# Issuing the row renewals of a tiled map iteration from GpSimd instead of from SyncE

## The chip, the cores and the metric

The kernel runs on one core of a Trainium2 chip. The time is device microseconds of one execution, and the runs of the kernel before have a median of 9524.16 us (three runs, 9523.93 to 9524.88 us). One more execution was taken under the hardware profiler; its page and trace are what is read below.

A core has a matrix engine (TensorE, PE in the profile; its weight loads are PEld), a vector engine (DVE), a scalar engine (ACT), GpSimd (POOL) and SyncE (SP). [...] SP computes nothing here: it issues transfers.

## What is computed

The input is `x`, 8 images of 8 channels of 512 x 512 floats. There are two layers, each with a residual. Layer 0 is a small spectral convolution of the group-normalised image, layer 1 is this:

```
drive = grid = normalised x
for _ in range(15):
    mapped = 3.9 * grid * (1 - grid)
    local  = conv3x3(mapped, one 3x3 kernel per channel)
    grid   = 0.85 * (0.7 * mapped + 0.3 * local) + 0.15 * drive
cml = clip(grid)
nca = sigmoid(conv1x1(relu(conv3x3(x, 8 -> 128)), 128 -> 8))
g   = sigmoid(conv1x1(relu(conv3x3([x, cml, nca], 24 -> 8))))
out = x + g * cml + (1 - g) * nca
```

The 15 steps of the map are the part that matters here. Each step needs, for each row, the rows above and below it.

## The kernel before, in words

**The map.** An image is cut by rows into slabs of 32 rows that lie 30 rows apart (`SLAB`, `PITCH`), so neighbouring slabs share two rows. A set (class `Slabs`) holds four slabs of four channels in one tile `m` of 128 partitions: four blocks of 32 partitions by four blocks of 514 floats. One of the two block indices is the slab and the other the channel, and they change places at each step, because the convolution of a step (line 524, 48 matmuls of 32 x 32 weights) moves a block from one index to the other. A half of an image (four channels) has four sets; the second half has a fifth, `Tail`, for the last rows. The first half of an image is one phase of 60 convolutions (4 sets by 15 steps), the second half one of 75 (5 by 15): 1080 in all. Within a phase the sets take turns, so a set is convolved at every fourth or fifth place.

After a convolution `settle` finishes the step: two DVE instructions add the drive and write `m` (line 537), two ACT instructions square it (line 543). In step 1 POOL scales the even drive (line 516, called from `drive`), in step 13 POOL adds 0.5 to the odd drive (line 547).

**The renewal.** A slab's first and last rows lack a neighbour, so after each of the first 14 steps they are wrong and are fetched from the neighbouring slab (`renew`). Lines 570 and 571 are one transfer each way: row 30 of a slab becomes row 0 of the next, row 1 of the next becomes row 31 of the slab. One such pair serves the slabs within a set; a second pair serves the border to the set above, and its line 571 writes into that set's tile. In odd steps the pair within a set copies three partitions of 2056 floats, in even steps four of 1542; the pair between sets copies one partition as 8 x 257, or four of 514. The tail set has its own `renew` (lines 637, 641, 646), which is not touched.

**A turn.** `turn` emits two convolutions with the rest of the work placed around them, 540 turns for the whole map. In `work` (line 1013) the order is: POOL scales the odd drive of sets that are due (line 516); convolution A; its two DVE instructions and the first square; `others.finish()` (line 821 on DVE and the store of line 828 on SP); convolution B; the rest of A's step, with A's renewals; B's two DVE instructions and first square; the loads of `transfers`; up to two rounds of the 128-channel convolution (line 723, read out by lines 729 and 731), in the first of which B's step ends, with B's renewals; the gate's convolution (line 793, with lines 798 on POOL and 803 on DVE); its second part (line 810, the sigmoid of line 814 on ACT, and line 816 on POOL). What line 816 makes is read by line 821 in the next turn, and line 723 of that turn follows line 821.

`keep_order` (line 102) makes each engine keep the order of the source. Every transfer of the main part is issued by SP, so its list mixes the renewals with the loads and stores; SP waits in turn for whatever the next transfer needs. Each transfer also carries one of eight completion semaphores, taken in rotation[...]. POOL's list in the map holds only lines 516, 547, 798 and 816.

Of the kernel before, what the change touches and what calls it, by code (L numbers as in the profile page):

```python
# [111 lines left out]
def view(t, offset, dims):  # L112

    return bass.AP(tensor=t.tensor, offset=t.offset + offset, ap=[list(d) for d in dims])
# [3 lines left out]
def conv_layers(ctx: ExitStack, tc: tile.TileContext, a, out):  # L118
    nc = tc.nc
# [350 lines left out]
    class Slabs:  # L470
# [84 lines left out]
        def renew(self, step):  # L555
            s, width = 4 * NP, (4 if step % 2 else 1) * NP
            m, above = self.m, self.above


            if step % 2:  # L560
                pairs = [(m, 0, m, 32 * s, [[32 * s, 3], [1, 4 * NP]])]
                if above:
                    pairs.append((above.m, 96 * s, m, 0, [[s, 1], [1, 4 * NP]]))
            else:
                pairs = [(m, 0, m, NP, [[32 * s, 4], [1, 3 * NP]])]
                if above:
                    pairs.append((above.m, 3 * NP, m, 0, [[32 * s, 4], [1, NP]]))
            for ta, oa, tb, ob, dims in pairs:
                ra, rb = oa + PITCH * s, ob
                nc.sync.dma_start(out=view(tb, rb, dims), in_=view(ta, ra, dims))  # L570
                nc.sync.dma_start(out=view(ta, ra + s, dims), in_=view(tb, rb + s, dims))
            if self.k == SETS - 1:
                r, past = TAIL_AT - (4 * SETS - 1) * PITCH, self.e.past[step]
                past = past[self.c0 : self.c0 + 4]
                if step % 2:
                    past = past.rearrange("(a c) w -> a c w", a=1)
                    row = m[96 + r : 97 + r, :, 1 : N + 1]
                else:
                    row = view(m, r * s + 3 * NP + 1, [[32 * s, 4], [1, N]])
                nc.sync.dma_start(out=past, in_=row)  # L580
# [377 lines left out]
    for i in range(3):  # L958
        xn = dram.tile([NP + 1, C, N], F32, name=f"xn{i}")
        cml, nca = (dram.tile([NP, C, N], F32, name=f"{name}{i}") for name in ("cml", "nca"))  # L960
        for plane in (xn, cml, nca):
            nc.scalar.dma_start(
                out=view(plane, 0, [[(NP - 1) * C * N, 2], [N, C], [1, N]]), in_=zrow
# [185 lines left out]
```

## Time and profile before

| | |
|---|---|
| median of the runs | 9524.16 us |
| the profiled execution: its own time / its span | 9539.07 us / 9537.3 us |
| PE busy | 9076.3 us, 95% |
| DVE, ACT, POOL busy | 5572.4, 4071.8 and 1671.2 us |
| line 570, line 571 | 1568 transfers each, issued by SP, median 0.645 and 0.631 us of SP each |
| all transfers issued by SP | 7496 |
| lines 547, 798, 816 on POOL | 72, 344 and 344 instructions of 5.37, 1.28 and 1.27 us |

The span runs from the first to the last instruction of the profiled execution. Busy time of an engine does not count its waiting. [...] its busy share says how long it had something in hand, not how near it is to its peak. The time in which an engine was idle is put down to whatever released it. The transfers that SP issues show only the time that the issue held SP; the bytes move later, as packets of the queue.

### The profile page before, as it was taken

To read this page: it belongs to the slowest core of one execution; us is meant where nothing else is said; L and a number is where in the kernel's file an instruction comes from. 1 tells how busy PE (TensorE), PEld (TensorE's weight loads), DVE (VectorE), ACT (ScalarE), POOL (GpSimd) and SP (SyncE) were. 2 spreads that over 40 slices of the span, in tenths; PEclk is the share of its full clock that TensorE was granted. 3 is DMA by queue.
4 is the path that set the end of the run, shared out by engine and by line. 5 is a ranking of instruction groups with operands and counts; after the bars stand their busy time and mean duration, and the time that the engine had idled before them with its cause. 6 is when DMAs were issued, how large, how long until landed. Compare 5 with 4: busy or idle time off the path is not lost. (4 is left out here: it accounts for less than half of the span.)

```text
span 9537.3 us, 330619 instructions
## 1 busy us (share of the span) xinstructions
PE 9076.3 (95%) x148976; PEld 4075.3 (43%) x148976; DVE 5572.4 (58%) x5820; ACT 4071.8 (43%) x4285; POOL 1671.2 (18%) x1286
## 2 busy tenths in 40 slices
PE   6999999999999999999999999999999999888999
PEld 3444444444444444444444444444444444333433
DVE  5665566655665556655566555665556655454555
ACT  2444444444444444444444444444434444333432
POOL 2010111112121121211212121021211212122122
PEclk9999999999999999999999999999999999999999
DMA  4241365565555555555555546555464555565288
GB/s 146 87 127 35 90 165 137 148 142 137 157 152 142 140 130 146 160 133 136 153 135 162 146 117 172 131 158 133 120 175 131 156 142 123 138 157 139 70 203 196
DMA packets 626870, 1326.71 MB, mean 139 GB/s; under 512 B 75258, under 2 KB 80762, under 8 KB 597970
## 3 DMA queue, kind: packets, MB, share of 16 engines
q1 hardware_dynamic: 623104, 1304.42, 53.5%
q8 instruction: 1170, 19.17, 0.9%
q14 instruction: 242, 1.98, 0.1%
q10 hardware_dynamic: 2354, 1.14, 0.0%
HBM read 977.48 MB, written 270.61 MB: 131 GB/s over the span
## 5 line engine op out<-in xcount | busy, mean ns | idle before, releaser
L524 PE MATMUL pair<-m,band 32*32 32x512 f32 x103680 | 3719.4, 607 | 208.7 <-issue 124.1
L543 ACT ACTIVATE m<-m 128x1024 f32<-128x1024 f32 x2016 | 2124.5, 1055 | 2438.6 <-DVE m L537 2293.2
L723 PE MATMUL pair<-cols,w_p 32*128 32x511 f32 (+1 forms) x24576 | 2860.0, 603 | 44.8 <-ACT y L749 14.4
L524 PEld LDWEIGHTS pair<-m,band 32*32 32x32 f32 x103680 | 2005.0, 103 | 1856.4 <-issue 1052.5
L537 DVE SCALAR_TENSOR_TENSOR m<-pair,dO 128x1024 f32<-128x1024 f32 x1152 | 1356.6, 1219 | 1218.4 <-PE pair L524 973.3
L723 PEld LDWEIGHTS pair<-cols,w_p 32*128 32x128 f32 x24576 | 1310.0, 186 | 1612.4 <-issue 1158.8
L537 DVE SCALAR_TENSOR_TENSOR m<-pair,dE 128x1024 f32<-128x1024 f32 x1008 | 1187.0, 1219 | 1142.4 <-PE pair L524 902.9
L731 DVE TENSOR_SCALAR h<-pair,b_p 128x1024 f32<-128x1024 f32 x1024 | 1313.0, 1283 | 877.8 <-PE pair L723 873.4
L729 ACT ACTIVATE h<-pair,b_p 128x1024 f32<-128x1024 f32 x1024 | 1140.6, 1114 | 902.5 <-PE pair L723 902.1
L816 POOL TENSOR_TENSOR mix<-mix 96x512 f32<-96x512 f32 x344 | 438.0, 1273 | 4302.2 <-ACT mix L814 4053.3
L742 PE MATMUL pair<-h,w_u 128*32 128x512 f32 x8192 | 1059.1, 610 | 47.6 <-ACT h L729 47.5
L793 PE MATMUL pair<-gin,w_g 128*32 128x511 f32 (+1 forms) x8256 | 964.7, 600 | 4.0 <-DMA gin<-nca 2.0
L798 POOL TENSOR_TENSOR mix<-mix 96x512 f32<-96x512 f32 x344 | 442.2, 1285 | 1423.4 <-DMA mix<-nca 1134.4
L547 POOL TENSOR_SCALAR dO<-dO 128x2048 f32<-128x2048 f32 x72 | 394.5, 5491 | 1009.4 <-DVE m L537 1009.1
L742 PEld LDWEIGHTS pair<-h,w_u 128*32 128x32 f32 x8192 | 244.1, 110 | 698.1 <-issue 329.2
L755 ACT ACTIVATE y<-y,b_u 128x512 f32<-128x512 f32 x256 | 184.8, 722 | 816.9 <-DVE y L751 816.9
L793 PEld LDWEIGHTS pair<-gin,w_g 128*32 128x32 f32 x8256 | 234.5, 110 | 684.6 <-issue 463.1
L749 ACT COPY y<-pair 128x512 f32<-128x512 f32 x256 | 150.1, 586 | 634.4 <-PE pair L742 487.2
L803 DVE TENSOR_SCALAR mix<-pair,b_g 128x512 f32<-128x512 f32 x344 | 258.2, 750 | 263.0 <-PE pair L793 262.5
L810 PE MATMUL pair<-mix,w_g 128*32 128x512 f32 x2064 | 370.7, 605 | 41.9 <-DVE mix L803 38.9
L821 DVE SCALAR_TENSOR_TENSOR mix<-mix,back 96x512 f32<-96x512 f32 x344 | 313.5, 911 | 144.2 <-POOL mix L816 144.2
L516 POOL TENSOR_SCALAR dO<-dO,base 128x512 f32<-128x512 f32 x288 | 208.4, 741 | 1075.6 <-DMA dO<-xn 923.9
(87 smaller groups left out, 2632.2 us busy)
## 6 DMA issues: line engine op xcount, KB each, us to landing
gin<-xn SPq DMA_DIRECT2D x344, 384.0 KB
cols<-xn SPq DMA_DIRECT2D x256, 512.0 KB
x<-in_x SPq DMA_DIRECT2D x120, 1024.0 KB
gin<-cml SPq DMA_DIRECT2D x344, 320.0 KB
gin<-nca SPq DMA_DIRECT2D x344, 320.0 KB
dE<-xn SPq DMA_DIRECT2D x288, 256.0 KB
dO<-xn SPq DMA_DIRECT2D x288, 256.0 KB
mix<-xn SPq DMA_DIRECT2D x344, 192.0 KB
```

The source lines that it names most:

```text
L524: nc.tensor.matmul(ps[h // 2][32 * t : 32 * t + 32, h % 2], band[at, self.channel(step - 1, h, t), dx], m[at, t, dx : dx + N], start=(n == ...
L537: nc.vector.scalar_tensor_tensor(u[:, at], ps[q], FLOOR, d[:, at], ALU.max, ALU.add)
L543: nc.scalar.square(u[:, at], u[:, at])
L547: nc.gpsimd.tensor_scalar(d, d, 0.5, None, ALU.add)
L723: nc.tensor.matmul(ps[g // 2][:, g % 2, lo:hi], w_p[p, dx, i % 2], self.cols[p, i // 2, at : at + hi - lo], start=(n == 0), stop=(n == 2), ...
L729: nc.scalar.activation(h[:, :2], ps[0], AF.Relu, bias=b_p)
L731: nc.vector.tensor_scalar(h[:, 2:], ps[1], b_p, 0.0, ALU.add, ALU.max)
L742: nc.tensor.matmul(ps[32 * g : 32 * g + 32], w_u[:, r % 4], h[:, g], start=(r == self.hs[0][0]), stop=(r == self.hs[-1][0]), tile_position ...
L793: nc.tensor.matmul(ps[32 * j : 32 * j + 32, lo:hi], gband[:, dx], gin[:, j, at : at + hi - lo], start=(n == 0), stop=(n == 2), tile_positi ...
L798: nc.gpsimd.tensor_tensor(d, d, ng, ALU.subtract)
L810: nc.tensor.matmul(ps[at], gpoint[:, at], mix[:, 3], start=True, stop=True, tile_position=(0, 32 * j),)
L816: nc.gpsimd.tensor_tensor(d, d, mix[: GR * C, 2], ALU.mult)
```

## The change

Lines 570 and 571 are issued by GpSimd. What is copied, the tiles, the order in which the renewals come and all other transfers stay.

```
@@ -567,8 +567,8 @@
                     pairs.append((above.m, 3 * NP, m, 0, [[32 * s, 4], [1, NP]]))
             for ta, oa, tb, ob, dims in pairs:
                 ra, rb = oa + PITCH * s, ob
-                nc.sync.dma_start(out=view(tb, rb, dims), in_=view(ta, ra, dims))
-                nc.sync.dma_start(out=view(ta, ra + s, dims), in_=view(tb, rb + s, dims))
+                nc.gpsimd.dma_start(out=view(tb, rb, dims), in_=view(ta, ra, dims))
+                nc.gpsimd.dma_start(out=view(ta, ra + s, dims), in_=view(tb, rb + s, dims))
             if self.k == SETS - 1:
                 r, past = TAIL_AT - (4 * SETS - 1) * PITCH, self.e.past[step]
                 past = past[self.c0 : self.c0 + 4]
```

The built programs differ in two lists only: SP's loses 3136 transfers, POOL's gains them, in among lines 516, 547, 798 and 816 where the source emits them. The renewals then have eight completion semaphores of their own, and the eight of SP's transfers are left to the other 4360.

More of the change, by code (lines that the diff above doesn't have):

```diff
@@ L569, in renew @@
                 ra, rb = oa + PITCH * s, ob
-                nc.sync.dma_start(out=view(tb, rb, dims), in_=view(ta, ra, dims))
-                nc.sync.dma_start(out=view(ta, ra + s, dims), in_=view(tb, rb + s, dims))
+                nc.gpsimd.dma_start(out=view(tb, rb, dims), in_=view(ta, ra, dims))
+                nc.gpsimd.dma_start(out=view(ta, ra + s, dims), in_=view(tb, rb + s, dims))
             if self.k == SETS - 1:
```

## The prediction

> **What bounds the kernel now.** The page first: busy time of each engine, then its costliest groups.
>
> ```profile
> PE 9076.3 (95%) x148976; PEld 4075.3 (43%) x148976; DVE 5572.4 (58%) x5820; ACT 4071.8 (43%) x4285; POOL 1671.2 (18%) x1286
> ...
> L547 POOL TENSOR_SCALAR dO<-dO 128x2048 f32<-128x2048 f32 x72 | 394.5, 5491 | 1009.4 <-DVE m L537 1009.1
> ```
>
> PE has something in hand for 95% of the span. Little can be won beside it, and whatever holds PE up is lost for good. POOL is idle for 9537 - 1671 = 7866 us, but its line 547 is long: 5.5 us at a time.
>
> Next, PE's own waits.
>
> ```profile
> PE pair L524 <- issue: 124.1, 79, 4.3
> ...
> PE pair L524 <- DMA m<-m: 37.3, 9, 11.1
> ```
>
> Columns: us in total, times, longest. Renewals (`m<-m`) hold PE for 37.3 us in all: 9 waits, among them one of 2.7 to 11.1 us at the start of each of the seven later images. No other transfer holds PE in the map. That is all that faster renewals can give directly: 0.4%.
>
> One of these waits in the timeline (start, us):
>
> ```profile
> 1177.57 1.05 ACT L543 ACTIVATE m<-m 128x1024 f32<-128x1024 f32 x1
> ...
> 1178.57 0.68 SPq L570 DMA_DIRECT2D m<-m  x1
> 1179.30 1.24 SPq L571 DMA_DIRECT2D m<-m  x1
> 1180.59 0.92 SPq L570 DMA_DIRECT2D m<-m  x1
> 1181.55 1.02 SPq L571 DMA_DIRECT2D m<-m  x1
> ...
> 1187.91 3.09 PE L524 MATMUL pair<-m,band 32*32 32x512 f32 x43 [6.13 <-DMA m<-m]
> ```
>
> SP had been issuing something else until 1178.5 us (a store, line 758, that it held from 1171.0), so renewals whose data were squared at 1174.0 us left late; the last one landed 6.3 us after its issue.
>
> Elsewhere there is slack. Each renewal's packets are recognisable by size (8224, 6168, 2056 and 1028 bytes); from issue to the end of its last packet is 2.0 us at the median, 9.7 at the 99th percentile. From there to the matmul that needs it is 22 us at the median; in the phases of four sets, for the row written into the set above, 11, and under 4.3 in one case of 20.
>
> Last, the other side: what waits for POOL.
>
> ```profile
> DVE mix L821 <- POOL mix L816: 144.2, 43, 8.1
> ```
>
> And a turn of step 13, with two line 547 in a row:
>
> ```profile
> 2218.16 11.12 POOL L547 TENSOR_SCALAR dO<-dO 128x2048 f32<-128x2048 f32 x2 [3.65 <-DVE m L537]
> ...
> 2228.12 0.67 ACT L814 ACTIVATE mix<-pair,b_g 96x512 f32<-96x512 f32 x1
> ...
> 2229.25 1.27 POOL L816 TENSOR_TENSOR mix<-mix 96x512 f32<-96x512 f32 x1
> ...
> 2233.18 0.74 DVE L821 SCALAR_TENSOR_TENSOR mix<-mix,back 96x512 f32<-96x512 f32 x1
> ...
> 2234.01 2.43 PE L723 MATMUL pair<-cols,w_p 32*128 32x512 f32 x20
> ```
>
> Line 816 already starts late here (the sigmoid ended at 2228.79), and ends 2.66 us before line 821 starts. PE's line 723 comes right behind line 821, and so does convolution B's read-out on DVE: a late line 816 is a late PE.
>
> [...] this trace shows 1.1 us at least and 1.4 at the median from SP's issue to the first packet. [...] The trace has no transfer issued by POOL[...]. [...]
>
> **The change part by part.**
>
> *Taken from SP.* 3136 issues of some 0.64 us, 2.0 ms, and SP's waits for line 543 (1275.6 us at line 570). SP is on PE's path only where it is late: the 37.3 us. The loads of a turn go out about 2.6 us earlier (four issues); PE waits for none of them in the map, so nothing.
>
> *Added to POOL.* 3136 issues at c us each. The trace does not give c. From below: SP's fastest, 0.49 us[...]. [...] POOL is then busy 1671 + 3136 = 4807 us, half the span; it would be full at c = (9537 - 1671)/3136 = 2.5 us.
>
> *Line 816 behind the renewals.* Of the 540 turns, 224 have eight renewals. In a common turn they cost nothing: B's are ready near the middle of the turn (2508.7 in the turn of 2500 to 2516 us), eight at 1.0 us fit in before the sigmoid that line 816 waits for (2518.04), and line 821 leaves it another 2 us. In the quoted turn they don't fit. POOL is never idle there: 11.12 for line 547 twice, 8c, 1.27 for line 816, from 2218.16: it ends at 2230.55 + 8c, and line 821 is late by 8c - 2.63 us: 5.4 at c = 1. That goes to line 723 and PE. I laid POOL's new list, in its new order, along the trace: an instruction starts when its input is there (the end of line 543, 537 or 814, or its old start) and POOL is free, and each delay of line 821 shifts what follows. At c = 1.0, 15 of 344 executions of line 821 are late, by 47.8 us in all; over 0.5 us it is late once or twice per image, always in or behind step 13 with its line 547, by 7.4 us at most. At c = 0.5 it is 8.8 us, at 0.8, 29; at 1.2, 73; at 1.5, 151; at 2.0, 600.
>
> *Renewals behind POOL's work.* They wait for lines 516, 547, 798 and for each other: 1.35 us at the median at c = 1, 12 at the 99th percentile, inside the slack above. With 2 to 3 us from issue to landing (the old median, and 1 more), convolutions wait 7 to 10 us more, chiefly in step 14 of the last phase, where turns are short. [...] faster landing is not counted.
>
> *The waits of 37.3 us.* In the same laying-out the renewals are ready early enough to save 34 us: in the quoted case they leave POOL by 1178.2 us. Of the longest, 11.1 us, 7.8 are saved; the others go whole.
>
> *Lines 516 and 547 behind renewals.* Their outputs are needed a step or two later, one or two rounds of sets (30 us and more); lost cover would show as DVE waiting for line 516, 21.1 us now. Nothing.
>
> Sum at c = 1.0: +47.8 + 7 (to 10) - 34 = +21 to +24; some spare for what I left out, +25. On the profiled execution: 9539.07 + 25 = 9564. The runs lie 15 us below it: 9524.16 + 25 = 9549, taken as 9550.
>
> **The rivals.**
>
> *Faster: POOL's issue is as cheap as SP's.* At c = 0.5 the sum is 8.8 + 0 - 35 = -26: 9498. It decides below c = 0.7 (-10). For it: a renewal has only 3 to 8 pieces, SP needs 0.64 us. [...] At c = 0.8 the sum is 0: the change is a wash between 0.7 and 0.95.
>
> *Much slower: POOL becomes the bound.* At c = 1.5: 151 + 45 - 31 = +165, 9690; at 2.0: 599 + 135 - 23 = +711, 10235. Common turns then overflow: eight issues are 12 to 16 us of a turn of some 16. For it: nothing in the trace excludes it. [...]
>
> *No change: the renewals were hidden and stay hidden.* For it: 22 us of slack. Against: seven turns in which they were not, and line 816, which is not a renewal. The change does what it says: the built lists show it.
>
> **How the numbers follow.** A measurement of this kernel can tell about 0.2%, 19 us, from no change. Cheap issue, c under 0.7: 22%, 9490 to 9515. Wash, c of 0.7 to 0.95: 20%, 9514 to 9540. The forecast, c of 0.95 to 1.35: 43%, 9533 to 9620 (at 1.3: 90 + 23 - 33 = +80), its lowest tenth within 0.2%. Beyond 1.35: 15%. Thus faster 0.23, same 0.25, slower 0.52. The range leaves out the cheapest few per cent and those over c = 1.4 (+118 to 131): 9494 to 9645.
>
> **What would show it.** POOL busy near 4800 us, its rows for lines 570 and 571 near 1.0 us; PE's wait for `m<-m` down from 37.3 to under 12 us; DVE's wait of line 821 for line 816 up from 144 by some 50, in turns with line 547; line 828 on SP waiting as before. The forecast fails if c is not near 1.0, if landings from POOL take over 5 us[...].

## The result, and the profile after

The changed kernel takes 9490.16 us (median of 7 runs, 9478.60 to 9497.38), the kernel before beside it 9524.88 us (7 runs, 9509.79 to 9534.68). The ratio is 0.9963, 95% interval 0.9951 to 0.9974: faster by 0.37%, some 35 us. The prediction was 9550 us with a range of 9494 to 9645, so it had the sign wrong. The profiled execution took 9485.99 us, its span is 9484.2 us.

The page of the changed kernel: busy time of each engine, then groups (busy us, mean ns of one, idle before them).

```profile
PE 9052.0 (95%) x148976; PEld 4062.8 (43%) x148976; DVE 5647.2 (60%) x5820; ACT 4078.4 (43%) x4285; POOL 3362.1 (35%) x4422
...
L570 POOL DMA_DIRECT2D m<-m x1568 | 864.1, 551 | 3929.1 <-ACT m L543 3853.4
...
L571 POOL DMA_DIRECT2D m<-m x1568 | 844.9, 539 | 30.0 <-issue 25.9
...
L547 POOL TENSOR_SCALAR dO<-dO 128x2048 f32<-128x2048 f32 x72 | 391.9, 5443 | 112.4 <-DVE m L537 111.4
```

A renewal holds POOL for 0.545 us at the mean, not 1.0: POOL is busy for 1691 us more, not 3136. DVE, which the change gave nothing to do, is busy for 75 us more. Most of that is line 799, the DVE instruction that comes behind line 798 and now often runs beside it: its time over 0.73 us an instruction sums to 74.6 us in the map, 10.9 before. No wait of PE shows a loss from it, and the fastest kernel below has nearly as much of it (71.3).

The waits of the changed kernel (us in total, times, longest):

```profile
DVE mix L821 <- POOL mix L816: 152.8, 52, 9.2
...
PE pair L524 <- issue: 105.7, 72, 3.7
...
PE pair L723 <- DVE m L537: 16.4, 6, 3.3
...
PE pair L524 <- DMA m<-m: 13.5, 8, 4.0
```

PE's wait for renewals fell from 37.3 to 13.5 us. Most of line 821's wait lies after the map has ended: within the map it is 8.4 us, where no such wait is listed before. New is PE's line 723 waiting for line 537, 16.4 us (4.2 before).

The image start that the prediction showed, now from the changed kernel's timeline (start us, duration us):

```profile
1160.91 8.16 SPq L758 DMA_DIRECT2D nca<-y  x1
...
1170.00 0.54 POOL L570 DMA_DIRECT2D m<-m  x1 [0.38 <-ACT m L543]
1170.53 0.51 POOL L571 DMA_DIRECT2D m<-m  x1
...
1180.73 1.87 PE L524 MATMUL pair<-m,band 32*32 32x512 f32 x45
```

SP is held by the store of line 758 as before (8.16 us), but the renewals leave POOL 0.4 us after their square. From this convolution to the next it is 8.9 us (1171.8 to 1180.7); before it was 17.1 (1180.7 to 1197.8). Compared convolution by convolution (the start of each in one kernel against the same one in the other), the seven later image starts gain 46 us together (5.0 to 8.2 each).

The same view has what is lost, in the turn of step 13 that the prediction quoted:

```profile
2212.18 0.67 ACT L814 ACTIVATE mix<-pair,b_g 96x512 f32<-96x512 f32 x1
...
2217.56 1.28 POOL L816 TENSOR_TENSOR mix<-mix 96x512 f32<-96x512 f32 x1
...
2218.80 5.37 POOL L547 TENSOR_SCALAR dO<-dO 128x2048 f32<-128x2048 f32 x1
2218.87 4.12 DVE L821 SCALAR_TENSOR_TENSOR mix<-mix,back 96x512 f32<-96x512 f32 x1 [1.54 <-POOL mix L816]
...
2224.18 5.51 PE L723 MATMUL pair<-cols,w_p 32*128 32x512 f32 x24 [3.26 <-DVE m L537]
```

Line 816 is late behind the eight renewals, and line 821 waits 1.54 us for it: that was foreseen. Line 821 then takes 4.12 us instead of 0.74, because its late start puts it next to a line 547 on POOL: that was not. In the map this happens seven times, each time 0.07 or 0.08 us after a line 547 began. The loss is handed to PE.

Line 821 was not always short in the kernel before (durations in ns: least, median, greatest):

```profile
L821 DVE SCALAR_TENSOR_TENSOR mix<-mix,back x344: 737/739/1859, 1240.2 to 9533.1; 96x512 f32<-96x512 f32 x172
```

In 52 of the map's 301 executions it ran beside line 798, and took up to 1.86 us; in the map of the changed kernel it meets line 798 nowhere. What it takes over 0.74 us an instruction sums to 21.0 us in the map before and 25.1 after: seven long ones in place of many shorter ones.

### The profile page after: what moved, and what is told of

It reads as the page before. It is cut to its first block, busy times and chain, and to the rows that moved or that the text cites. A ratio compares the mean times of both kernels' runs of the same rounds, so it can differ in the third digit from the quotient of the medians.

```text
span 9484.2 us, 331791 instructions
## 1 busy us (share of the span) xinstructions
PE 9052.0 (95%) x148976; PEld 4062.8 (43%) x148976; DVE 5647.2 (60%) x5820; ACT 4078.4 (43%) x4285; POOL 3362.1 (35%) x4422
## 5 line engine op out<-in xcount | busy, mean ns | idle before, releaser
L723 PE MATMUL pair<-cols,w_p 32*128 32x511 f32 (+1 forms) x24576 | 2854.9, 603 | 59.8 <-DVE m L537 16.4
L570 POOL DMA_DIRECT2D m<-m x1568 | 864.1, 551 | 3929.1 <-ACT m L543 3853.4
L571 POOL DMA_DIRECT2D m<-m x1568 | 844.9, 539 | 30.0 <-issue 25.9
```

The lines of the kernel that those rows point to most:

```text
L570: nc.gpsimd.dma_start(out=view(tb, rb, dims), in_=view(ta, ra, dims))
L571: nc.gpsimd.dma_start(out=view(ta, ra + s, dims), in_=view(tb, rb + s, dims))
L723: nc.tensor.matmul(ps[g // 2][:, g % 2, lo:hi], w_p[p, dx, i % 2], self.cols[p, i // 2, at : at + hi - lo], start=(n == 0), stop=(n == 2), ...
```

## The experiments

Ratios are to the kernel before, run beside each set; its medians were 9516.89 us for the four kernels up to the longer line 547, 9526.12 for the two that follow and the two of the last pair, and 9522.94 for the two between these. The first four ran on one chip, the others on another; each kernel has 4 to 14 runs. Kernels with a new tile have their lines two further down (line 547 is 549, line 821 is 823); where the issuing engine is chosen per step, what follows it lies one further.

**Where the gain comes from: the renewals of step 1 alone, and all but those.**

```
-                nc.sync.dma_start(...)
+                q = nc.gpsimd if step == 1 else nc.sync     # first kernel
+                q = nc.sync if step == 1 else nc.gpsimd     # second kernel
+                q.dma_start(...)
```

> Only the renewals of step 1 (224 of 3136) are issued by GpSimd, the others by SP as before. Theory A, the gain is that these few leave SP's clogged queue at the start of a phase: PE's wait for m<-m falls from 37 us to under 10, and the time is 30 to 45 us under the kernel before, as good as the whole change or better, since POOL's cost in step 13 is gone. Theory B, the gain is SP's shorter list, so that loads leave earlier: 7% of the issues are moved, so 2 or 3 us.

> The reverse: step 1 stays with SP, the other 2912 renewals are issued by GpSimd. Theory A: PE's wait for m<-m stays at 30 to 40 us, POOL's cost in step 13 remains (8 us of waiting for line 816, 24 us of a longer line 821), so 0 to 25 us over the kernel before. Theory B: about 32 us under it.

Measured: step 1 alone 9486.77 us, ratio 0.9963 [0.9950, 0.9975]; the rest 9522.43 us, 1.0001 [0.9993, 1.0009]. PE's wait for renewals in the first:

```profile
PE pair L524 <- DMA m<-m: 7.9, 4, 3.7
```

and in the second:

```profile
PE pair L524 <- DMA m<-m: 51.7, 13, 10.0
```

224 of 3136 renewals, the ones at the image starts, bring as much as all of them. The reading at this point was that the other 2912 bring nothing. That was too quick, as the kernels with a short line 547 show further down: they bring two things of opposite sign.

**What POOL's time costs: twice as many issues.**

```
+                n = dims[-1][1] // 2
+                for at in (0, n):
+                    some = [*dims[:-1], [1, n]]
+                    nc.gpsimd.dma_start(out=view(tb, rb + at, some), in_=view(ta, ra + at, some))
...
```

> Each renewal is issued by GpSimd as two transfers of half the columns, so POOL pays two issues of 0.54 us, 1.09 us for what cost 0.545. This is the price that the prediction had taken. If the prediction's laying-out is right, line 821 then waits about 60 us for line 816, convolutions wait 10 to 25 us more, and the time is 35 to 60 us over the kernel before (9560 to 9585). If POOL has room for it, the time stays that of the change, 35 us under the kernel before.

Measured: 9621.09 us, 1.0105 [1.0088, 1.0123], 100 us over the kernel before and more than the laying-out gave. An issue stays at 0.55 us, POOL is busy for 5005.8 us. Waits of this kernel (line 573 and 574 issue, 821 and 826 are the former 816 and 821):

```profile
POOL m L573 <- DMA m<-m: 282.4, 194, 6.8
...
POOL m L574 <- DMA m<-m: 273.8, 234, 4.6
...
DVE mix L826 <- POOL mix L821: 267.6, 111, 8.5
...
PE pair L524 <- DMA m<-m: 59.6, 36, 5.5
```

Line 821's wait is there as the prediction describes it (124.3 us of it within the map). But POOL also waits for earlier renewals to land, 556 us in all. The trace names the semaphores: 425 of these 428 waits are for the one that the waiting issue itself carries. POOL's transfers take eight of them in turn: in the changed kernel 392 transfers carry each, and every one had landed 2.8 us or more before the next issue that carried the same. The laying-out had no such wait; so this kernel confirms the path to PE, and is no clean measure of its size.

**Line 547: longer, then shorter.** In the quoted turn POOL's renewals, line 816 and line 547 stand in one row. The first kernel was meant to shorten line 547 (theory: its one-operation form is the slow one). It takes the form for that of line 516, but subtracts where line 516 adds:

```
-                nc.gpsimd.tensor_scalar(d, d, 0.5, None, ALU.add)
+                nc.gpsimd.tensor_scalar(d, d, 1.0, mhalf, ALU.mult, ALU.subtract)
```

> The change, with line 547 written as d * 1.0 - (-0.5) with the constant in a tile, the form of line 516, which takes 2.0 us for the same 2048 floats where line 547 takes 5.4. If the form sets the duration, line 547 falls to 2.0 us, line 821 no longer waits for line 816 nor takes 4.1 us beside line 547, and the time is 10 to 25 us under the change. If the duration comes from what runs beside it, it stays at 5.4 us and the time at that of the change.

Measured: 9551.91 us, 1.0038 [1.0024, 1.0052]. This form is slower still, by the groups of that kernel:

```profile
L547 POOL TENSOR_SCALAR dO<-dO,mhalf 128x2048 f32<-128x2048 f32 x72 | 519.6, 7216 | 96.5 <-DVE m L537 94.9
```

The expectation failed, but the run tells something: 72 x 1.8 = 128 us more on an engine that is idle for two thirds of the time cost about 70 us (1.0038 - 0.9963 = 0.75%); its runs have a granted TensorE clock (as a share of full speed) of 0.980 to 0.983, against 0.984 to 0.986 with the change, which may be part of that. In the map, line 821 now takes 5.06 us ten times, each time beside a line 547. The second kernel takes exactly line 516's form:

```
+    phalf = cp.tile([P, 1], F32, name="phalf")
+    nc.vector.memset(phalf, 0.5)
...
-                nc.gpsimd.tensor_scalar(d, d, 0.5, None, ALU.add)
+                nc.gpsimd.tensor_scalar(d, d, 1.0, phalf, ALU.mult, ALU.add)
```

> The change, with line 547 written as d * 1.0 + 0.5, the 0.5 read from a 128 x 1 tile: the very form of line 516, which takes 2.0 us for 2048 floats, against 5.37 us of the form with an immediate add. Everything else as in the change. Theory C (line 547 is what the change still pays for: line 816 stands behind it and the renewals, and line 821 runs long beside it): line 547 near 2.0 us, POOL busy some 240 us less than in the change (72 x 3.4), line 821 no longer longer than 2 us anywhere, its waits for line 816 within the map near 0, and a time 15 to 40 us under the change, that is a ratio to the kernel before of 0.992 to 0.995. Rival (the change's remaining losses lie elsewhere, at the conflict of 798 with 799 or in the later landings): line 547 shorter, but the time as the change's within 10 us, ratio 0.9955 to 0.997. If line 547 does not get shorter with this form, the run says nothing on either.

Measured: **9440.05 us, ratio 0.9906 [0.9891, 0.9921]**, the fastest of all: 50 us under the change, more than expected. Line 547 in its groups:

```profile
L549 POOL TENSOR_SCALAR dO<-dO,phalf 128x2048 f32<-128x2048 f32 x72 | 150.2, 2087 | 191.8 <-DVE m L539 190.5
```

The same turn in its timeline:

```profile
2216.43 0.66 ACT L816 ACTIVATE mix<-pair,b_g 96x512 f32<-96x512 f32 x1
...
2217.18 1.27 POOL L818 TENSOR_TENSOR mix<-mix 96x512 f32<-96x512 f32 x1 [2.18 <-ACT mix L816]
...
2221.50 0.74 DVE L823 SCALAR_TENSOR_TENSOR mix<-mix,back 96x512 f32<-96x512 f32 x1
2221.69 2.39 POOL L549 TENSOR_SCALAR dO<-dO,phalf 128x2048 f32<-128x2048 f32 x1 [3.23 <-DVE m L539]
```

POOL is now idle for 2.18 us ahead of this turn's line 818 (the former 816) and ends it 3 us before it is needed; line 823 takes 0.74 us, and nowhere more than 1.74. Compared with the changed kernel convolution by convolution, the map's last one starts 39 us earlier. Seven places give 38 us of it, 3.6 to 6.9 us each: the seven turns in which the changed kernel has a line 821 of 4.12 us. The ups and downs elsewhere sum to 1 us.

**The short form without the other renewals.**

> Only the renewals of step 1 on GpSimd (224 of 3136, the rest on SP), with the same form of line 547 as in the run before. Theory C holds that line 547 costs time only where renewals stand between it and line 816; in this kernel the step-13 renewals are SP's, so 0 to 10 us under the kernel with step 1 alone: ratio to the kernel before 0.995 to 0.9965. Rival (a line 547 of 5.4 us costs by itself, through the vector engine beside it, also without renewals on POOL): over 15 us under it, ratio under 0.995.

> The kernel before, all renewals on SP, with only the form of line 547 changed (2.0 us in place of 5.37). Theory C (line 547's length costs only where renewals stand between it and line 816): 0 to 10 us under the kernel before, ratio 0.999 to 1.0005. Rival (the 50 us that this form took off the change come from line 547 itself, wherever the renewals are issued): 30 to 50 us, ratio 0.995 to 0.997.

> The other 2912 renewals (all but step 1's) on GpSimd, with the short form of line 547. With the long form these renewals gave nothing (ratio 1.0001). Theory D (they gave two things that cancelled: a gain of some 40 us over the whole map and stalls of line 821 in the turns of step 13): with the stalls gone the gain shows, ratio 0.9945 to 0.997, although PE's wait for renewals stays near 50 us because step 1 is still SP's. Rival (they give nothing by themselves, and the best version needs all renewals off SP): ratio above 0.998.

Measured: with step 1 on GpSimd 9485.22 us, 0.9944 [0.9926, 0.9961]; with all renewals on SP 9512.44 us, 0.9990 [0.9980, 0.9999]; with all but step 1 on GpSimd 9480.50 us, 0.9956 [0.9944, 0.9969]. The short form takes 10 us off the kernel before, as theory C expects where no renewals stand on POOL. What it takes off the kernel with step 1 alone is less certain: 1.5 us by the medians, 18 by the ratios. The ratio 0.9944 lies in the rival's range and its interval reaches into theory C's; two of the six runs (9449.36 and 9465.93 us) lie 17 us and more under the others. The run with all renewals on SP decides between the two. And the other renewals do bring a gain once the long line 547 is out of their way. Together with the others:

| on GpSimd | line 547 as it was (5.4 us) | short form (2.0 us) |
|---|---|---|
| none | 1 | 0.9990 |
| step 1 (224) | 0.9963 | 0.9944 |
| all but step 1 (2912) | 1.0001 | 0.9956 |
| all (3136) | 0.9963 | 0.9906 |

Read downwards, step 1 is worth 0.37 to 0.50% (35 to 48 us) in every pairing. The other 2912 are worth nothing with the long line 547, and 0.34 to 0.38% (32 to 36 us) with the short one. Read across, the short form is worth 0.10 to 0.19% where the other renewals are SP's, 0.45 to 0.57% where they are POOL's: the stalls in the step-13 turns cost the difference, some 35 us. So the change holds three terms: about -35 (image starts), about -35 (the other renewals), about +35 (step 13). Single entries are uncertain by 0.1 to 0.2%, so the terms are good to 10 to 20 us.

What the -35 of the other renewals is made of is not settled. With step 1 still on SP, PE's wait for renewals does not fall:

```profile
PE pair L526 <- DMA m<-m: 45.4, 11, 10.3
```

The gain is spread over the map. PE's idle time without a visible cause is 20 us less than with the short form alone (131.3 to 110.9 us). Its busy time is 20 us less too (9059.4 to 9039.5 us), but the granted clock was 0.986 in place of 0.983 in these two executions; if it followed the clock, the ratio of the clocks alone would give some 28 us (an estimate: 9059.4 x 0.003 / 0.986), so the busy time tells nothing. Among runs at a clock of 0.984 the gain is 25 us (median 9511.0 us of 5 runs, 9486.0 of 2).

The traces hold one candidate. With the short form alone, line 821 is lengthened beside line 798, as in the kernel before, by 20.7 us in the map; with the other renewals ahead of line 798 in POOL's list the two no longer meet, and it is 1.3 us. The 27 turns in which line 821 lost over 0.3 us gain 15 of the 38 us by which the map is shorter. As many turns picked at random gain 4 us on average and now and then 25, so this is a hint; no run separates it.

**Why step 1's renewals were late: the store, SP's list, or something shared.** Here those of step 1 go to ACT's list, which is not SP's either, and then only the store of line 758 goes to GpSimd:

```
+                q = nc.scalar if step == 1 else nc.sync     # first kernel, lines 571 and 572
...
-                    nc.sync.dma_start(                      # second kernel, line 758
+                    nc.gpsimd.dma_start(
```

> Only the renewals of step 1 are moved, and to the scalar engine's queue instead of GpSimd's: again a list that is not SP's[...]. Theory A1 (what the seven image starts gained is the place in line: the renewals no longer stand behind a store and bulk loads in SP's list): the wait of PE for renewals in the map falls to 8 to 12 us as with step 1 on GpSimd and the ratio is 0.996 to 0.998, the scalar engine losing 224 x 0.65 = 146 us of its idle time, some of it ahead of line 543's squares. Rival A2 [...]: at the image starts the scalar engine's issues take several us each, the wait of PE for renewals stays above 25 us, and the ratio is 0.999 or more.

> The kernel before, all renewals on SP, but the store of line 758 (which held SP for 6.6 to 7.5 us at four of the seven image starts) issued by GpSimd. Theory S1 (that store holds SP because of what it itself waits for or how many pieces it has; without it SP is free for the renewals): at those four starts the renewals leave at their squares' ends, the wait of PE for renewals falls from 37 to some 15 to 22 us, ratio 0.997 to 0.9985. Rival S2 (SP's list is held [...], and whatever comes next is held): the next issue after the loads takes 6 to 7 us in its place, the waits stay at 30 us or more, ratio 0.9995 to 1.001.

Measured: ACT 9626.44 us, 1.0103 [1.0088, 1.0118]; the store 9528.90 us, 1.0003 [0.9995, 1.0011]. Neither theory foresaw the first: PE's wait for renewals fell as one has it, to 5.3 us, and yet the kernel lost 100 us. PE now waits for ACT (lines 743 and 730 are the former 742 and 729; this wait was 47.5 us before):

```profile
PE pair L743 <- ACT h L730: 133.9, 117, 18.4
...
PE pair L524 <- DMA m<-m: 5.3, 2, 5.2
```

Its timeline at one image start:

```profile
2343.26 0.69 ACTq L571 DMA_DIRECT2D m<-m  x1
...
2351.91 0.68 ACTq L572 DMA_DIRECT2D m<-m  x1
...
2355.61 0.67 ACTq L571 DMA_DIRECT2D m<-m  x1
2356.32 0.64 ACTq L572 DMA_DIRECT2D m<-m  x1
2357.01 2.00 ACT L543 ACTIVATE m<-m 128x1024 f32<-128x1024 f32 x2 [15.85 <-DMA m<-m]
```

An issue takes 0.7 us, but ACT stands still for 8 us between two of one pair, and for 3 us more before the next; ACT is idle for 15.85 us ahead of the square behind them. What it waits for can be read from the trace, which names the semaphores. ACT's and SP's transfers carry the same eight, those of GpSimd eight others. In the kernel before, SP's 7496 issues take theirs in turn, 936 to 938 each, and 7319 of them stand behind a wait for the very one that they carry. The issue at 2351.91 carries the one that a store of SP's (line 601, the former 600), issued at 2333.41, had carried before it, and starts 0.02 us after the last update of that semaphore, so after the store's landing. The issue at 2355.61 starts in the same way 0.02 us after the landing of a gate load of SP's, issued at 2344.71. In all, ACT waits 25 times for the semaphore that its own issue carries, 67.4 us together; every wait of over 2.6 us is one for a transfer of SP's.

Three image starts lose 13.6 to 16.2 us at one convolution, 45 us together, and win some of it back just after. The starts of seven second phases lose 4.8 to 15.3 us, 63 together; there the waits for semaphores are 2.6 us at most, and what else ACT's issues delay is not worked out. SP's own hold does not reach ACT: while SP's store of line 759 (the former 758) was held for 8.35 us from 2334.73, ACT issued two renewals at 2336.09 and 2336.86, in 0.74 and 1.25 us.

The second, SP's timeline where before line 758 had been held for 7.83 us behind the stores of line 600 (the expectation counts four such image starts; they are six of the seven, with 6.6 to 7.8 us):

```profile
2325.17 7.88 SPq L600 DMA_DIRECT2D cml<-m  x6
2333.15 6.81 SPq L570 DMA_DIRECT2D m<-m  x1
```

With the store gone, the next in the list, now a renewal, is held for 6.81 us; at the seven image starts it is 2.9 to 7.4 us. So it is what stands ahead of it, line 600, that holds SP; the store was only next in line. How these stores hold SP is not shown. PE's wait stays:

```profile
PE pair L524 <- DMA m<-m: 35.9, 8, 11.0
```

## Why the prediction was wrong

**The step that failed** is the cost c of an issue on POOL. The forecast is worked out at c = 1.0 us. That was the author's estimate; the trace of the kernel before has no transfer issued by POOL and did not show it. How long the issue holds POOL and when the transfer's packets move are two different things. POOL was held for 0.545 us at the mean, less than SP before (0.60). The first packet of a renewal came 1.07 us after the issue at the least and 2.4 at the median, and its last packet ended 3.6 us after the issue at the median (3.0 for line 570, 4.3 for line 571), against 2.0 from SP. The rival "Faster: POOL's issue is as cheap as SP's" was the true case; its price, 9498 us, is 8 us from the median. With c = 0.545 the prediction's own figures, read between those for 0.5 and 0.8, give about 12 us of stalls and 35 saved: -23 against the measured -35 (interval -25 to -47). That this comes so near is in part luck, as what follows shows.

**It does not follow that the rest of the working was right.** Two terms were missing, and they cancel.

- *"PE waits for none of them in the map, so nothing"* (SP relieved of 2912 renewals): with the short line 547 their move brings 32 to 36 us. Only the rows in which PE waits for a transfer were read for it. Part of the gain shows in PE's idle time without a visible cause; whether it comes from SP's shorter list, from line 798's later place in POOL's, or from both, is open.
- *GpSimd's work lengthening DVE's*, for which the forecast counts nothing: line 821 (DVE, `mix` from `mix` and `back`) takes 0.74 us by itself, 4.12 beside a line 547 of 5.37 that began first. It was not held to the end of line 547, though: it ended 1.2 us before it. Seven times 3.38 us makes 24 us, beside 8.4 us of plain waiting: 32 of the some 35 us of step 13.

**What held.** PE as the bound; the waits of 37.3 us as what step 1 can give (34 predicted as saved; 24 us by that row, 46 by the convolutions' starts, 35 by the time of step 1 alone). The formula for the quoted turn: 8c - 2.63 = 1.7 us at 0.545, measured 1.54. The place of the loss, "in or behind step 13 with its line 547", is that of all seven. Landings were later than the 2 to 3 us of the laying-out: 3.6 us at the median to the last packet, which is how the prediction counts, 8.2 at the 99th percentile (9.7 before), and 4.7 (line 570) and 5.8 us (line 571) to the last update of the semaphore. They did no harm that shows: PE waits less for renewals than before.

**How firm the 35 us are.** Among runs with the same granted clock, 0.985, the kernel before has a median of 9511.5 us (11 runs), the changed one 9490.7 (4 runs): 21 us. The other 14 come with a clock that is 0.984 to 0.986 in the changed kernel and 0.982 to 0.985 before. Whether the change causes that is open.

## What to carry to other kernels

Before a queue is changed, separate three prices: how long the issue holds its engine (here 0.545 us on GpSimd, 0.60 on SP), how long until it lands (3.6 us to the last packet against 2.0), and what it waits for in line (here up to 7.8 us behind SP's stores). The gain at the image starts came from the third. A second list was worth it for these renewals on GpSimd (ratio 0.9963), which shared neither the line nor the completion semaphores with the bulk transfers, and not on ACT (1.0103), which shared the semaphores. Moving work onto an idle engine can make its long instructions expensive: line 547 cost 0.1 to 0.2% while no other renewals stood in POOL's list, and 0.5% once they did, so shorten the long ones together with the move. A result of zero can be two terms that cancel; cross the factors before calling a part worthless.

## What the runs showed of the hardware

- The same 2048 floats per partition in place on GpSimd, plus one half: 5.37 us as one add of an immediate, 7.17 as times 1.0 minus a value from a tile, 1.98 as times 1.0 plus a value from a tile.
- A VectorE instruction with two tiles as inputs (line 821) went from 0.74 us to 4.12 beside a GpSimd instruction of 5.37 us that had begun 0.07 or 0.08 us earlier, and to 5.06 beside one of 7.16 us; beside a GpSimd instruction of 1.28 us it took up to 1.86.
- Behind bulk stores SP was held for 6.6 to 7.8 us at its next transfer in the kernel before, for 2.9 to 7.4 with another transfer in that place.
- A small transfer held GpSimd for 0.545 us at the mean; its last packet ended 3.6 us after the issue at the median, and its semaphore was complete about 1.1 us later.
- Transfers issued by ACT carried the same eight completion semaphores as SP's, and ACT stood still for 8 us in the middle of a pair until a store of SP's had landed; those issued by GpSimd carried eight others, and in the changed kernel each had landed 2.8 us or more before the next issue with the same one.
